# Layer 1 of a two-layer kernel: row gathers with a bound, and PSUM operands for VectorE's additions

## The chip, the cores and the metric

The kernel runs on one core of a Trainium2 chip. The metric is the time of one execution on the device in microseconds, as the median of several. The times in the profile come from one execution taken by the hardware profiler. Engine names in the profile: PE is the matrix multiplier (TensorE), PEld its loading of weights, DVE is VectorE, ACT is ScalarE, POOL is GpSimd, SP the engine that issues most DMAs; a small q (ACTq, SPq) is the queue of an engine. L853 is line 853 of the kernel.

## The reference

The input is 32 images of 128 channels and 56 x 56 pixels, all in float32. There are two layers.

Layer 0 is a depthwise 7 x 7 convolution and a layer norm over the channels, followed by a mixture of eight experts. Each of the T = 32 x 56 x 56 = 100,352 pixels is a token, and chooses its two best experts. An expert takes at most `cap = 1.25 T / 8 = 15,680` choices, in the order of the first choice's weight; what comes later is dropped and gets slot `E * cap`, which is a row of zeros:

```python
pos = take_along_axis(cumsum(oneh, axis=0) - 1, tiF[:, None], axis=1)[:, 0]
keep = pos < cap
slot = where(keep, tiF * cap + pos, E * cap)
y = einsum('ecf,efd->ecd', gelu(einsum('ecd,edf->ecf', eb, W1) + b1), W2) + b2
yf = concatenate([y.reshape(E * cap, C), zeros((1, C))], axis=0)
contrib = yf[slot] * gate[:, None]      # two rows of yf for each token
x = input + x_skip + layer_scale * (contrib summed over the two choices)
```

Layer 1 takes this x. It makes `feat`, a dilated 3 x 3 convolution down to 64 channels with batch norm and gelu, and its two-dimensional Fourier transform F2. One half of the output's channels is the absolute value of the inverse transform of an attention over the channels, the other that of the inverse transform of F2 times a sigmoid gate. Both are added to x:

```python
out_f = abs(ifft2(einsum('bhde,bhen->bhdn', attn, F2)))
gate = abs(ifft2(sigmoid(...) * F2))
return concatenate([out_f, gate], axis=1) + x
```

## The kernel before

There are three stages, one after the other. The first makes the convolution of layer 0, the norm and the choice of experts, and writes the normed tokens to `xf` in DRAM. The second lists the tokens of each expert, gathers them (`xg`, L674) and runs the experts; their rows, already multiplied by gate and layer scale, go to `yf` in DRAM. `yf` has NSLOT = 125,440 rows and one more, which is filled with zeros from `zrow` (L389 to L391). `slot1` and `slot2` hold for each token the row of its first and second choice, or NSLOT where the choice was dropped. The third stage is layer 1, and the change lies there.

The third stage works on pairs of images, sixteen of them. The image pair is laid out as two padded tiles `xps[0]`, `xps[1]` of 128 channels, and `feat` holds both images' 64 channels in 128 partitions. Two generators are woven together. `front` makes the x of the next pair and its `feat`; `back` does the Fourier part of the present pair. The main loop runs a step of `front` whenever `back` has done its share of matmul columns (`goal`). The order of instructions on each engine is fixed when the kernel is built; it follows this weaving roughly, not line by line.

`front` goes over seven row blocks of a pair (r counts them over all pairs, 112 in all). For each block there are four things:

- `gather(r)` loads seven times 128 tokens of `xf` as `xs` (L848), and for each of the two choices seven gathers of 128 rows from `yf` into a tile `y` (L853). A gather is an indirect DMA that GpSimd issues; its row numbers are one column of `slot1` or `slot2`. The `y` tiles come from a pool of four, so two blocks are in flight.
- `total(r)` adds the two `y` tiles to `xs` on VectorE (L867), which frees them.
- `place(r)` transposes `xs` on TensorE into PSUM (`pxs`, L875) and adds it into `xps` on VectorE (L880).
- `taps` does the 3 x 3 convolution as matmuls (`pf`, L898), with gelu on ScalarE into `feat` (L906).

`feed(rb)` in `front` calls `place(r)`, `total(r + 1)` and `gather(r + 3)` in that order.

`back` has four transforms, each of which transposes (`pt`, L934), copies to SBUF on VectorE (`mid`, L936), multiplies (`pm`, L942) and copies out, mostly on ScalarE (L945, L1020). Between the second and the third stand the attention weights (`gb`, `at_`, `attn`) and seven calls of `attend(g)`: two matmuls `pre` and `pim` (L1032, L1033), a square of each on ScalarE into `sr` and `si` (L1036, L1037), and the addition of both on VectorE into `feat` (L1038). There too lie the gate (`gt`, L1088) and the sums and differences X, Y and Q (L1057 to L1061, L1091 to L1097). Beside the third transform, `attended(g)` takes the root of `feat` on ScalarE for each image into `oa` (L1046), adds x on VectorE (L1049) and stores. After the fourth transform, `absolute` takes the absolute value of each image's half of `pm` on ScalarE into `ob` (L1122), adds x on VectorE (L1126) and stores.

[...] Here `bank(...)` hands out five of them in turn for `pt`, `pm`, `pre`, `pim`, `pxs` and the like; a bank is free again when its last reader is done.

Of the kernel before, what the change touches and what calls it, by code (L numbers as in the profile page):

```python
# [29 lines left out]
F32 = mybir.dt.float32  # L30
I32 = mybir.dt.int32
AF = mybir.ActivationFunctionType
ALU = mybir.AluOpType
# [4 lines left out]
C = 128  # L38
H = W = 56
RP = 59  # L40
XL = 62 * RP + 6
NQ = H * RP
INT0 = 3 * RP + 3
# [3 lines left out]
DD = 64  # L47
# [3 lines left out]
NB = H // P8  # L51
# [8 lines left out]
def interior(ap, h0, nh):  # L60

    at = INT0 + h0 * RP
    return ap[:, at : at + nh * RP].rearrange("p (h w) -> p h w", w=RP)[:, :, 0:W]
# [8 lines left out]
def conv_seq_kernel(ctx: ExitStack, tc: tile.TileContext, t: dict, out: bass.AP, dbg: dict):  # L72
    nc = tc.nc
# [4 lines left out]
    NSLOT = E * cap  # L78
# [5 lines left out]
    dram = ctx.enter_context(tc.tile_pool(name="dram", bufs=1, space=DRAM))  # L84
# [3 lines left out]
    def bank(name):  # L88
        return psum.tile([128, 512], F32, tag="bank", name=name)
# [10 lines left out]
    nc.vector.memset(eps6, 1.0e-6)  # L100

    xf = dram.tile([J * 128, PITCH], F32, name="xf")
    yf = dram.tile([NSLOT + 1, C], F32, name="yf")
    xfv = xf.rearrange("(j p) c -> p j c", p=128)


# [7 lines left out]
    with tc.tile_pool(name="a1", bufs=1) as a1, tc.tile_pool(name="a2", bufs=2) as a2, tc.tile_pool(  # L114
        name="a3", bufs=3
# [214 lines left out]
        for g in range(HI // 2):  # L330
            y = a2.tile([128, TG, C], F32, name="y")
# [31 lines left out]
    with tc.tile_pool(name="b1", bufs=1) as b1, tc.tile_pool(name="b2", bufs=2) as b2, tc.tile_pool(  # L363
        name="c1", bufs=1
# [21 lines left out]
            )  # L386
            nc.vector.tensor_tensor(out=b2v[:, e], in0=b2v[:, e], in1=lsB, op=ALU.mult)

        zrow = c1.tile([1, C], F32, name="zrow")  # L389
        nc.vector.memset(zrow, 0.0)  # L390
        nc.sync.dma_start(out=yf[NSLOT : NSLOT + 1, :], in_=zrow)  # L391

        blocks = b1.tile([128, U, NC], F32, name="blocks")
        for u in range(U):
            nc.vector.tensor_scalar(
                out=blocks[:, u, :], in0=iota[:, :NC], scalar1=float(-u), scalar2=None, op0=ALU.add
# [4 lines left out]
            out=token, in0=iota, scalar1=-128.0, scalar2=128.0, op0=ALU.add, op1=ALU.mult  # L401
# [397 lines left out]
    d2 = ctx.enter_context(tc.tile_pool(name="d2", bufs=2))  # L799
# [42 lines left out]
    rows = {}  # L842

    def gather(r):
        if r >= NRB:
            return
        xs = d3.tile([128, NB, C], F32, name="xs")
        nc.sync.dma_start(out=xs, in_=xfv[:, r * NB : (r + 1) * NB, :C])  # L848
        ys = []
        for s in (slot1, slot2):  # L850
            y = d4.tile([128, NB, C], F32, name="y")
            for m in range(NB):
                nc.gpsimd.indirect_dma_start(  # L853
                    out=y[:, m, :],
                    out_offset=None,
                    in_=yf,
                    in_offset=bass.IndirectOffsetOnAxis(ap=s[:, r * NB + m : r * NB + m + 1], axis=0),
                )
            ys.append(y)
        rows[r] = xs, ys  # L860

    def total(r):
        if r >= NRB:
            return
        xs, ys = rows[r]
        for y in ys:
            nc.vector.tensor_tensor(out=xs, in0=xs, in1=y, op=ALU.add)  # L867

    def place(r, xps):
        xs, rb = rows.pop(r)[0], r % NB  # L870
        for m0 in range(0, NB, 4):
            nm = min(4, NB - m0)
            pt = bank("pxs")
            for m in range(nm):
                nc.tensor.transpose(pt[:, m * 128 : (m + 1) * 128], xs[:, m0 + m, :], ident)  # L875
            pv = pt[:, : nm * 128].rearrange("p (m i r s) -> p i r m s", m=nm, i=2, r=P8)
            for i in range(2):
                px = interior(xps[i], rb * P8, P8)[:, :, m0 * P8 : (m0 + nm) * P8]
                px = px.rearrange("p r (m s) -> p r m s", m=nm)
                nc.vector.tensor_tensor(out=px, in0=px, in1=pv[:, i], op=ALU.add)  # L880

    def front(pr, xps, feat):


        for i in range(2):
            nc.sync.dma_start(out=xps[i], in_=t["xp"][pr + i * HI])

        def feed(rb):
            r = pr * NB + rb
            place(r, xps)  # L890
            total(r + 1)
            gather(r + 3)

        def taps(pf, g, k0):
            for k in range(k0, k0 + 3):
                o = ((k // 3) * 3 + 8 * g) * RP + (k % 3) * 3
                for i in range(2):
                    nc.tensor.matmul(  # L898
                        pf[i * DD : (i + 1) * DD, : 8 * W],
                        lhsT=cw[:, k, :],  # L900
                        rhs=xps[i][:, o : o + 8 * RP].rearrange("p (h w) -> p h w", w=RP)[:, :, :W],
                        start=(k == 0),
                        stop=(k == 8),
                    )
            if k0 == 6:
                nc.scalar.activation(  # L906
                    feat[:, 8 * g * W : 8 * (g + 1) * W], pf[:, : 8 * W], AF.Gelu, scale=bsc, bias=bsh
                )

        feed(0)  # L910
        yield NB * 64
        for g in range(NB):
            if g + 1 < NB:
                feed(g + 1)
                yield NB * 64
            pf = psumf.tile([128, 512], F32, name="pf")
            for k0 in (0, 3, 6):
                taps(pf, g, k0)
                yield 3 * 8 * W


# [37 lines left out]
    def back(pr, xps, feat):  # L959
# [67 lines left out]
        def attend(g):  # L1027

            pre = bank("pre")
            pim = bank("pim")  # L1030
            ftf = feat[:, 8 * g * W : 8 * (g + 1) * W]
            nc.tensor.matmul(pre[:, : 8 * W], lhsT=attn, rhs=ftf, start=True, stop=True)  # L1032
            nc.tensor.matmul(pim[:, : 8 * W], lhsT=meanw, rhs=ftf, start=True, stop=True)  # L1033
            sr = d2.tile([128, 8 * W], F32, name="sr")
            si = d2.tile([128, 8 * W], F32, name="si")
            nc.scalar.activation(sr, pre[:, : 8 * W], AF.Square)  # L1036
            nc.scalar.activation(si, pim[:, : 8 * W], AF.Square)  # L1037
            nc.vector.tensor_tensor(out=ftf, in0=sr, in1=si, op=ALU.add)  # L1038
            return 2 * 8 * W

        def attended(g):

            for i in range(2):
                oa = ring.tile([128, 8 * W], F32, name="oa", tag="o")
                ov = oa[:DD].rearrange("p (h w) -> p h w", w=W)
                nc.scalar.activation(  # L1046
                    oa[:DD], feat[i * DD : (i + 1) * DD, 8 * g * W : 8 * (g + 1) * W], AF.Sqrt
                )
                nc.vector.tensor_tensor(out=ov, in0=ov, in1=interior(xps[i], 8 * g, 8)[:DD], op=ALU.add)  # L1049
                nc.sync.dma_start(out=out[pr + i * HI, :DD, 8 * g : 8 * g + 8, :], in_=ov)  # L1050


# [51 lines left out]
        for i, w in enumerate(  # L1104
            transform(
                lambda k: Q[:, 2 * k : 2 * k + 2, :].rearrange("p a l -> p (a l)"), KF, 4 * KF, ih,
                lambda k, n: T4[:, 2 * k * H : 2 * (k + n) * H], act,
            )
        ):
            if i % 2 and i // 2 < NB:  # L1110
                attended(i // 2)
            yield w
# [3 lines left out]

        def absolute(at, pm):
            j0, nj = at
            for i in range(2):
                ob = ring.tile([128, 8 * W], F32, name="ob", tag="o")  # L1120
                ov = ob[DD:].rearrange("p (b j w) -> p b j w", b=2, w=W)
                nc.scalar.activation(  # L1122
                    ov, pm[i * DD : (i + 1) * DD].rearrange("p (j b w) -> p b j w", b=2, w=W), AF.Abs
                )
                px = xps[i][DD:, INT0 : INT0 + H * RP].rearrange("p (b j w) -> p b j w", b=2, w=RP)
                nc.vector.tensor_tensor(out=ov, in0=ov, in1=px[:, :, j0 : j0 + nj, :W], op=ALU.add)  # L1126
                po = out[pr + i * HI, DD:].rearrange("c (b j) w -> c b j w", b=2)
                nc.sync.dma_start(out=po[:, :, j0 : j0 + nj, :], in_=ov)

        yield from transform(  # L1130
            lambda j: T4[:, bass.DynSlice(j, 4 * KF, step=NT)], NT, 4 * KF, iw,
            lambda j, n: (j, n), absolute,
        )

# [6 lines left out]
    for r in range(3):  # L1141
        gather(r)
# [9 lines left out]
    for w in front(0, *this):  # L1152
        pass
    for pr in range(NI // 2):
        then, steps = None, iter(())
        if pr + 1 < NI // 2:
            then = pair()
            steps = front(pr + 1, *then)
        made = fed = 0
        for w in back(pr, *this):  # L1160
            made += max(w, 0)
            goal = max(0, made - LEAD) * FRONT // (MAIN - LEAD)
            if w < 0:
                goal = max(goal, fed - w * 3 * 8 * W)
            while fed < goal:
                f = next(steps, None)
                if f is None:
                    break
                fed += f
        for w in steps:  # L1170
            pass
        this = then
# [137 lines left out]
```

## Time and profile before

| | before |
|---|---|
| median of 3 runs | 5500.93 us (5497.88 to 5509.63) |
| span of the profiled execution | 5513.8 us |
| stage 3, from the first gather of `y` to the end | 3250.2 to 5513.8 us |
| gathers of `y` (L853) | 1568, mean 1045 ns, busy 1638.6 us |
| additions `xs<-xs,y` (L867) | 224, mean 1091 ns |
| `oa<-oa,xp` (L1049) and `ob<-ob,xp` (L1126) | 224 each, mean 612 and 627 ns |
| `feat<-sr,si` (L1038) | 112, mean 619 ns |
| roots (L1046) and absolute values (L1122) | 224 each, mean 576 and 538 ns |
| loads of ScalarE's table at L1046 in stage 3 | 79, 1283 ns each |

A line of the costliest groups reads: line, engine, operation, what is written from what, how often; then busy time and the mean of one; then the idle time of that engine just before these instructions, and what ended most of it. "issue" means that the engine waited for nothing that the profile shows. In the timeline, a line has the start in us, the length in us, the instruction, and in brackets the idle time before it. A line of the windows has, for each engine, busy time and number of instructions in that stretch, then the granted TensorE clock, the share of the DMA engines that is busy, and GB/s.

### The profile page before, as it was taken

What the parts mean: (1) busy time and instruction counts of PE and PEld (TensorE: products, weight loads), DVE (VectorE), ACT (ScalarE), POOL (GpSimd) and SP (SyncE); (2) the same over time, 40 slices, a digit from 0 to 9 for tenths busy, and PEclk for the clock granted to TensorE, in tenths of its full rate; (3) what the DMA queues carried; (4) which work ended last, traced back from release to release, by engine and by line L of the source; (5) the groups of instructions that cost most, each with busy time, mean ns of one, the idle gap of its engine ahead of it and who ended that gap; (6) DMA issues with size and microseconds to landing.
All of it is one profiled execution on the core that took longest, in us unless ns stands there. A gap on an engine that the chain in (4) does not pass through costs nothing.

```text
span 5513.8 us, 85629 instructions
## 1 busy us (share of the span) xinstructions
PE 4653.0 (84%) x32850; PEld 3226.8 (59%) x32850; DVE 3073.9 (56%) x6927; ACT 2097.5 (38%) x3595; POOL 2613.8 (47%) x2564
## 2 busy tenths in 40 slices
PE   6777675189988989899999965899999999899898
PEld 6666554166666667667776743555555555555556
DVE  4767776746565656454453322555555555555556
ACT  2544556023322323233333310444444444444445
POOL 0000000053535343445454447777777777777770
PEclk9888887589999999999999987999999999999999
DMA  9999995222222222222222243444444444444441
GB/s 258 247 242 244 241 233 132 50 66 60 69 54 66 57 62 61 63 66 71 69 70 73 73 120 74 118 126 127 123 123 124 125 123 123 125 128 125 123 121 42
DMA packets 616217, 634.09 MB, mean 115 GB/s; under 512 B 166145, under 2 KB 540546, under 8 KB 611714
## 3 DMA queue, kind: packets, MB, share of 16 engines
q1 hardware_dynamic: 332418, 395.64, 25.6%
q0 software_dynamic: 81664, 175.18, 14.8%
q10 hardware_dynamic: 201728, 57.81, 5.4%
q8 instruction: 260, 4.26, 0.3%
q14 instruction: 147, 1.20, 0.1%
HBM read 454.98 MB, written 173.41 MB: 114 GB/s over the span
## 4 chain that ended last, share of the span: by engine, by line
POOL 28%; PE 25%; issue 19%; DVE 7%; DMA 6%; ACT 2%; ACTq 0%; POOLq 0%; DVEq 0%; SPq 0%
POOL y L853 17%; POOL xg L674 10%; PE py L718 6%; PE ph L708 5%; PE pf L898 4%; PE pm L942 4%; DMA xg<-xf,ids 3%; DMA y<-yf,slot 2%; PE pt L934 2%; PE pg L966 1%; ACT y L181 1%; PE psa L136 1%; PE pxt L680 1%; DVE junk L419 1%; DVE y L187 1%
## 5 line engine op out<-in xcount | busy, mean ns | idle before, releaser
L853 POOL DMA_INDIRECT y<-yf,slot x1568 | 1638.6, 1045 | 527.7 <-issue 501.0
L674 POOL DMA_INDIRECT xg<-xf,ids x984 | 963.8, 979 | 1338.4 <-PE pxt L680 490.0
L711 ACT ACTIVATE hT<-ph,b1t 128x512 f32<-128x512 f32 (+1 forms) x992 | 676.1, 682 | 1428.8 <-PE ph L708 1402.6
L718 PEld LDWEIGHTS py<-W,hT 128*128 128x128 f32 x7872 | 950.8, 195 | 224.7 <-issue 155.1
L718 PE MATMUL py<-W,hT 128*128 128x128 f32 x7872 | 998.2, 281 | 75.4 <-DVE yo L731 69.8
L708 PE MATMUL ph<-xT,W 128*128 128x512 f32 (+1 forms) x1984 | 903.9, 595 | 0.2 <-DVE xT L694 0.2
L898 PE MATMUL pf<-xp,cw 128*64 128x448 f32 x4032 | 885.9, 566 | 0.9 <-DVE xp L880 0.8
L867 DVE TENSOR_TENSOR xs<-xs,y 128x896 f32<-128x896 f32 x224 | 244.4, 1091 | 644.7 <-DMA y<-yf,slot 591.9
L898 PEld LDWEIGHTS pf<-xp,cw 128*64 128x64 f32 x4032 | 289.0, 141 | 465.9 <-issue 439.7
L708 PEld LDWEIGHTS ph<-xT,W 128*128 128x128 f32 x1984 | 359.9, 193 | 336.4 <-issue 329.7
L136 PE MATMUL psa<-xt,wt 112*64 112x98 f32 x8192 | 413.1, 262 | 83.2 <-DMA wt<-in_wt_dram 74.9
L685 DVE SCALAR_TENSOR_TENSOR gat<-xg 128x4 f32<-128x4 f32 (+2 forms) x256 | 42.1, 164 | 785.0 <-DMA xg<-xf,ids 782.4
L136 PEld LDWEIGHTS psa<-xt,wt 112*64 112x64 f32 x8192 | 389.4, 146 | 121.4 <-issue 67.0
L936 DVE COPY mid<-pt 112x512 f32<-112x512 f32 (+3 forms) x480 | 305.3, 660 | 229.7 <-PE pt L934 229.0
L290 POOL MEMSET meta<- 128x1568 f32 x8 | 11.2, 1404 | 887.1 <-DMA xf<-meta 451.5
L181 ACT ACTIVATE y<-y,nb,sd 128x128 f32<-128x128 f32 x784 | 307.9, 482 | 119.1 <-issue 70.2
L945 ACT COPY T<-pm 128x464 f32<-128x464 f32 (+2 forms) x240 | 124.7, 520 | 404.7 <-PE pm L942 404.7
L144 DVE TENSOR_TENSOR y<-psa,dwbB 128x392 f32<-128x392 f32 x256 | 142.7, 563 | 232.8 <-PE psa L136 232.7
L731 DVE TENSOR_TENSOR yo<-py,b2t 128x512 f32<-128x512 f32 (+2 forms) x256 | 169.8, 666 | 112.1 <-PE py L718 111.3
L198 PE MATMUL pyt<-ident,y 128*128 128x128 f32 x784 | 137.8, 347 | 92.0 <-DVE nb L174 57.9
L680 PE MATMUL pxt<-ident,xg 128*128 128x128 f32 (+1 forms) x984 | 195.2, 280 | 11.0 <-DMA xg<-xf,ids 10.8
L1033 PE MATMUL pim<-feat,meanw 128*128 128x448 f32 x224 | 126.4, 651 | 92.2 <-ACT gt L1088 92.2
(376 smaller groups left out, 6185.1 us busy)
## 6 DMA issues: line engine op xcount, KB each, us to landing
xt<-in_x_dram SPq DMA_DIRECT2D x128, 784.0 KB
yf<-yo SPq DMA_DIRECT2D x240, 256.0 KB
xp<-in_xp_dram SPq DMA_DIRECT2D x32, 1832.0 KB
wt<-in_wt_dram SPq DMA_DIRECT2D x128, 448.0 KB
xs<-xf SPq DMA_DIRECT2D x112, 448.0 KB
xf<-y ACTq DMA_DIRECT2D x48, 1024.0 KB
y<-yf,slot POOLq DMA_INDIRECT x1568
out_dram<-oa SPq DMA_DIRECT2D x224, 112.0 KB
```

The source lines that it names most:

```text
L136: nc.tensor.matmul(ps[h * 64 : (h + 1) * 64, c * TG : (c + 1) * TG], lhsT=wt[:, c4 + c, b, :], rhs=xv[:, c4 + c, h, :, b * NB : b * NB + N ...
L181: nc.scalar.activation(yi, yi, AF.Identity, scale=sd[:, i : i + 1], bias=nb[:, i : i + 1])
L674: nc.gpsimd.indirect_dma_start(out=xg[:n, q, :], out_offset=None, in_=xf, in_offset=bass.IndirectOffsetOnAxis(ap=ids[:n, c0 + q : c0 + q + ...
L680: nc.tensor.transpose(pt[:, q * 128 : q * 128 + n], xg[:n, q, :C], ident[:n, :n])
L708: nc.tensor.matmul(ph[:, :ns], lhsT=W1[:, e, f * C : (f + 1) * C], rhs=xT[:, :ns], start=True, stop=True)
L711: nc.scalar.activation(hT[:, f, :ns], ph[:, :ns], AF.Gelu, bias=b1t[:, e, f : f + 1])
L718: nc.tensor.matmul(py[:n, q * C : (q + 1) * C], lhsT=hT[:, f, q * 128 : q * 128 + n], rhs=W2[:, e, f, :], start=(f == 0), stop=(f == FF // ...
L853: nc.gpsimd.indirect_dma_start(out=y[:, m, :], out_offset=None, in_=yf, in_offset=bass.IndirectOffsetOnAxis(ap=s[:, r * NB + m : r * NB + ...
L867: nc.vector.tensor_tensor(out=xs, in0=xs, in1=y, op=ALU.add)
L898: nc.tensor.matmul(pf[i * DD : (i + 1) * DD, : 8 * W], lhsT=cw[:, k, :], rhs=xps[i][:, o : o + 8 * RP].rearrange("p (h w) -> p h w", w=RP) ...
L936: dve(mid[:m, :ni, :].rearrange("p i c -> p (i c)"), pt[:m, : ni * 128])
L942: nc.tensor.matmul(pm[:, i * M : (i + 1) * M], lhsT=mid[:m, i, :], rhs=by, start=True, stop=True)
```

## The change

It has two parts, and one move.

The gathers get a bound: a row number above NSLOT - 1 is skipped instead of read, so a dropped choice moves nothing. What it leaves in `y` must then be zero, so ScalarE clears each `y` tile before its gathers. The row of zeros in `yf` and its writing go. The purpose is to spare the reads of dropped choices.

The squares of `pim`, the roots and the absolute values are written to PSUM rather than to SBUF: `pim` and `pm` in place, the roots into a bank of their own, `root`. VectorE's additions then read one operand from PSUM and one from SBUF. [...] a root or an absolute value is taken once over 128 partitions for both images, where it was taken twice over 64.

The move: `gather` is no longer called in `feed` but later, behind the first three taps of a row block, for the same block r + 3.

```diff
-    yf = dram.tile([NSLOT + 1, C], F32, name="yf")
+    yf = dram.tile([NSLOT, C], F32, name="yf")
...
-        zrow = c1.tile([1, C], F32, name="zrow")
-        nc.vector.memset(zrow, 0.0)
-        nc.sync.dma_start(out=yf[NSLOT : NSLOT + 1, :], in_=zrow)
...
             y = d4.tile([128, NB, C], F32, name="y")
+            nc.scalar.memzero(y)
             for m in range(NB):
                 nc.gpsimd.indirect_dma_start(
                     out=y[:, m, :],
                     out_offset=None,
                     in_=yf,
                     in_offset=bass.IndirectOffsetOnAxis(ap=s[:, r * NB + m : r * NB + m + 1], axis=0),
+                    bounds_check=NSLOT - 1,
+                    oob_is_err=False,
                 )
...
             total(r + 1)
-            gather(r + 3)
...
         feed(0)
         yield NB * 64
+        gather(pr * NB + 3)
...
                 taps(pf, g, k0)
+                if k0 == 0 and g + 1 < NB:
+                    gather(pr * NB + g + 4)
                 yield 3 * 8 * W
...
-            si = d2.tile([128, 8 * W], F32, name="si")
             nc.scalar.activation(sr, pre[:, : 8 * W], AF.Square)
-            nc.scalar.activation(si, pim[:, : 8 * W], AF.Square)
-            nc.vector.tensor_tensor(out=ftf, in0=sr, in1=si, op=ALU.add)
+            nc.scalar.activation(pim[:, : 8 * W], pim[:, : 8 * W], AF.Square)
+            nc.vector.tensor_tensor(out=ftf, in0=sr, in1=pim[:, : 8 * W], op=ALU.add)
...
+            root = bank("root")
+            nc.scalar.activation(root[:, : 8 * W], feat[:, 8 * g * W : 8 * (g + 1) * W], AF.Sqrt)
             for i in range(2):
                 oa = ring.tile([128, 8 * W], F32, name="oa", tag="o")
                 ov = oa[:DD].rearrange("p (h w) -> p h w", w=W)
-                nc.scalar.activation(
-                    oa[:DD], feat[i * DD : (i + 1) * DD, 8 * g * W : 8 * (g + 1) * W], AF.Sqrt
-                )
-                nc.vector.tensor_tensor(out=ov, in0=ov, in1=interior(xps[i], 8 * g, 8)[:DD], op=ALU.add)
+                rv = root[i * DD : (i + 1) * DD, : 8 * W].rearrange("p (h w) -> p h w", w=W)
+                nc.vector.tensor_tensor(out=ov, in0=rv, in1=interior(xps[i], 8 * g, 8)[:DD], op=ALU.add)
...
+            nc.scalar.activation(pm, pm, AF.Abs)
             for i in range(2):
                 ob = ring.tile([128, 8 * W], F32, name="ob", tag="o")
                 ov = ob[DD:].rearrange("p (b j w) -> p b j w", b=2, w=W)
-                nc.scalar.activation(
-                    ov, pm[i * DD : (i + 1) * DD].rearrange("p (j b w) -> p b j w", b=2, w=W), AF.Abs
-                )
...
-                nc.vector.tensor_tensor(out=ov, in0=ov, in1=px[:, :, j0 : j0 + nj, :W], op=ALU.add)
+                nc.vector.tensor_tensor(
+                    out=ov,
+                    in0=pm[i * DD : (i + 1) * DD].rearrange("p (j b w) -> p b j w", b=2, w=W),
+                    in1=px[:, :, j0 : j0 + nj, :W],
+                    op=ALU.add,
+                )
```

More of the change, by code (lines that the diff above doesn't have):

```diff
@@ L1121, in absolute @@
                 ov = ob[DD:].rearrange("p (b j w) -> p b j w", b=2, w=W)
-                nc.scalar.activation(
-                    ov, pm[i * DD : (i + 1) * DD].rearrange("p (j b w) -> p b j w", b=2, w=W), AF.Abs
-                )
-                px = xps[i][DD:, INT0 : INT0 + H * RP].rearrange("p (b j w) -> p b j w", b=2, w=RP)
-                nc.vector.tensor_tensor(out=ov, in0=ov, in1=px[:, :, j0 : j0 + nj, :W], op=ALU.add)
+                px = xps[i][DD:, INT0 : INT0 + H * RP].rearrange("p (b j w) -> p b j w", b=2, w=RP)
+                nc.vector.tensor_tensor(
[3 more added lines that the diff above has]
+                    op=ALU.add,
+                )
                 po = out[pr + i * HI, DD:].rearrange("c (b j) w -> c b j w", b=2)
```

## Prediction

> **What bounds the kernel now.** I read the page first (engines, slices, costliest groups), then the chain of waits in the stage that the change touches, then a table of that stage in windows, and last the timeline of single instructions.
>
> ```profile
> PE 4653.0 (84%) x32850; PEld 3226.8 (59%) x32850; DVE 3073.9 (56%) x6927; ACT 2097.5 (38%) x3595; POOL 2613.8 (47%) x2564
> ...
> L853 POOL DMA_INDIRECT y<-yf,slot x1568 | 1638.6, 1045 | 527.7 <-issue 501.0
> ```
>
> The whole-span shares point at TensorE. They mix three stages, though: only the third one, from 3250 us on, is changed, and there the second line matters: 1568 gathers of 1045 ns, with an idle time ahead of them that waits for nothing ("issue").
>
> ```profile
> core 0: us, PE busy (x) PEld busy (x) DVE busy (x) ACT busy (x) POOL busy (x), PEclk, DMA share, GB/s
> 3250.00:3500.00 250.00, 141.71 (x691) 78.29 (x692) 63.61 (x110) 34.94 (x53) 190.85 (x194) 0.75 0.38 93
> 4436.00:4569.00 133.00, 121.83 (x745) 73.82 (x745) 75.58 (x133) 59.56 (x93) 103.14 (x99) 0.96 0.50 126
> 4569.00:4703.00 134.00, 122.80 (x745) 74.13 (x745) 75.50 (x133) 59.52 (x93) 104.14 (x99) 0.95 0.50 125
> 5370.00:5514.00 144.00, 122.95 (x798) 87.43 (x798) 88.22 (x156) 78.14 (x129) 0.00 (x0) 0.91 0.18 41
> ```
>
> In the windows, one pair of images takes 133.4 us, fourteen times running. A pair has 98 gathers. From 3500 to 5367 us they start 1359.4 ns apart on average: 98 x 1.3594 = 133.2 us, which is the period itself. The gap ahead of each is 0.30 us and never shorter, so GpSimd has no slack at all. TensorE is next: 122 of 133.4 us, and its idle 10 us are mostly two waits per pair that go back to gathers (about 6 us until ScalarE's `gt` at L1088, held by `xs` adds on VectorE that wait for gathers; 3 us ahead of `pre`). VectorE waits 411.6 us in the fourteen pairs for gathers to land. Only the 147 us after the last gather are free of it.
>
> What sets the length of a gather? The timeline:
>
> ```profile
> 4575.72 0.59 DVE L1092 TENSOR_TENSOR Y<-Y,gt 128x421 f32<-128x421 f32 x1
> ...
> 4577.24 1.03 DVE L1094 TENSOR_TENSOR Q<-X 128x841 f32<-128x841 f32 x1
> ...
> 4577.43 1.65 POOL L853 DMA_INDIRECT y<-yf,slot  x1 [0.30 <-issue]
> ...
> 4585.58 3.38 DVE L1049 TENSOR_TENSOR oa<-oa,xp 64x448 f32<-64x448 f32 x6
> ...
> 4587.85 1.33 POOL L853 DMA_INDIRECT y<-yf,slot  x1 [0.30 <-issue]
> ...
> 4592.99 1.88 DVE L936 COPY mid<-pt 116x512 f32<-116x512 f32 x3
> ...
> 4594.20 0.94 POOL L853 DMA_INDIRECT y<-yf,slot  x1 [0.30 <-issue]
> ```
>
> The gather beside `Q<-X` (two inputs, both in SBUF) takes 1.65 us, the one beside `oa<-oa,xp` (again two in SBUF) 1.33, the one beside a copy out of PSUM 0.94. I counted this over the fourteen pairs, 1374 gathers: the 723 that overlap no VectorE instruction with two SBUF inputs take 943 ns each, with 0.3 us over that in all; the 651 that do carry the whole excess, 152 us. Shared out by overlap, it is 54.0 us to `xs<-xs,y` (L867), 25.7 to `oa<-oa,xp` (L1049), 17.4 to `ob<-ob,xp` (L1126), 14.2 to `feat<-sr,si` (L1038), and 40 to the X, Y and Q operations.
>
> [...] adds start some 2 us after the last gather of their tile has ended. So fewer bytes alone do not shorten these 943 ns. [...]
>
> **The change part by part.**
>
> *Operands in PSUM.* `feat<-sr,pim`, `oa<-root,xp` and `ob<-pm,xp` each read one input from PSUM instead of two from SBUF. Their 35 instructions a pair no longer lengthen gathers: 25.7 + 17.4 + 14.2 = 57.3 us over fourteen pairs, 4.1 a pair. VectorE's own time stays (0.61 to 0.63 us an add here; copies out of PSUM take 0.69 for 512 columns). The `xs` adds and the X, Y, Q operations stay, and so do their 94 us.
>
> *ScalarE.* Seven roots over 128 partitions replace fourteen over 64 (0.576 us each: -4.0 us a pair), seven absolute values replace fourteen (0.538: -3.8). The built order of instructions shows 131 table loads instead of 225, six fewer a pair: -7.5. Added: 14 clears of 128x896. ScalarE's copies take 0.25 us for 112 columns and 0.53 for 448, so 0.83 ns a column and about 0.90 us a clear: +12.6. Sum -2.7 on 59.5 us of 133: ScalarE is hidden before and after.
>
> *The wait that the clears add.* A gather now waits for a clear, and the clear stands in ScalarE's queue behind `xs` adds. Behind it in that queue are the copies `Q`, the squares and `gt`, for which TensorE waits. In before, a `y` buffer comes free 5.5 us or more (median 24) ahead of the first gather that reuses it, so about 0.9 us of clearing plus its place in the queue fits. The tightest place is the fourth row block of a pair: there the built order sets four clears between the four `Q` copies. The buffer is free 6.3 us ahead; the clear ends about 1.4 us after, and the last `Q` copy is delayed by about 2 us. Both hide as long as the gathers bound the pair. Moving `gather` behind the first taps only changes the order in which things are queued.
>
> *PSUM banks held longer.* `pm` is held by one activation and two adds (about 1.8 us) instead of two activations (1.1), and `root` takes a sixth user of five banks. A step of the transforms takes two banks, so TensorE runs about two steps ahead, some 3 us; it may lose a few us a pair, inside the 6 to 9 us that it gains when gathers come earlier.
>
> *The skip.* Choices: 2 x 100,352 tokens = 200,704; slots 8 x 15,680 = 125,440; so at least 37.5% of the rows, 48 of 128 in a gather, are skipped (from the shapes). Before, they all read the zero row. Their bytes weigh nothing, DMA is at half share. What counts is GpSimd's time per gather, and no gather of before has a bound. Low end: a skipped row costs as little as an absent one. The eight gathers of 64 rows in the second stage take 903 to 906 ns against 943 for 128: 40 ns for 64 rows, so 30 ns saved. [...] I take zero, a compare that eats what the skipped rows save.
>
> Each ns counts 1568 times, 1.57 us. Sum: 5500.9 - 57.3 + 0 = 5443.6. The pair goes to 129.2 us and is still GpSimd's: 98 x (1.013 + 0.305).
>
> **The rivals.**
>
> *Skipped rows shorten the gather by 30 ns.* Another 1568 x 0.030 = 47 us: 5397. The pair would be 126.3 us, just above what TensorE needs (133.4 less 10 idle, about 124), so little more can come. For it: rows cost something in the 64-row gathers. Against: little[...].
>
> *The bound costs 80 ns a gather.* +125 us: 5569, slower. [...]
>
> *The new waits take the gain.* Clears in ScalarE's queue or banks held longer stop TensorE, or gathers start late by about 4 us a pair: 5500, no change. For it: four clears between the `Q` copies. Against: ScalarE is 45% busy and the slack is 20 us in most places.
>
> **How the numbers follow.** 0.42 for the forecast, 0.25 for the shorter gather, 0.24 for the dearer one, 0.09 for the new waits. Predicted 5444. The range runs from 5385 (shorter gathers and a few us in the last 147) to 5575 (80 ns more)[...]. Faster: 0.42 + 0.25 + a third of the last = 0.70. Within 0.2%: 0.05. Slower: 0.25.
>
> **What would show it.** The mean of a gather: 1010 ns as forecast, 980 in the first rival, 1090 in the second. Its shortest: 943 if the test is free. The timeline beside `oa` and `ob`: 0.94 us gathers. The pair's window: 129 us with the 0.30 us gap before each gather. A gap that grows with ScalarE as its releaser would show the new waits, TensorE idle on ScalarE or VectorE the held banks. Wrong at the root would be gathers that stay long beside PSUM adds, or a length that has nothing to do with VectorE.

## The result, and the profile after

The changed kernel takes 5541.87 us (median of four executions, 5534.33 to 5551.94) where the kernel before takes 5499.68 on the same chip: a ratio of 1.0074, 95% interval 1.0054 to 1.0095. It is slower by about 42 us. The profiled executions are 28 us apart (5541.7 and 5513.8), because the one of before, an execution of 5515.6 us, was slower than any of its timed runs; traces are compared with those 28 us.

From the page of the changed kernel: the engines, the queue that carries the gathers, and the groups of the gather and of the clear (busy us, mean ns | idle us ahead and what ended most of it).

```profile
PE 4690.9 (85%) x32850; PEld 3232.8 (58%) x32850; DVE 3098.7 (56%) x6926; ACT 2040.4 (37%) x3501; POOL 2648.5 (48%) x2564
...
q0 software_dynamic: 81664, 136.94, 9.6%
...
L852 POOL DMA_INDIRECT y<-yf,slot x1568 | 1673.5, 1067 | 527.0 <-issue 469.0
...
L850 ACT ACTIVATE y<-y 128x896 uint32<-128x896 uint32 x224 | 212.3, 949 | 644.7 <-DVE xs L868 620.5
```

The skip does what it is for. The queue of the gathers moves 136.94 MB instead of 175.18; 38.24 MB at 512 bytes a row are 74.7 thousand rows not read, some 37% of them. And yet a gather has become longer on average, 1067 ns instead of 1045. The idle time ahead of the gathers is what it was (527.0 and 527.7 us): nothing new is waited for. The waits of GpSimd in the last stage say so directly (us in total, times, longest us):

```profile
POOL y L852 <- issue: 419.3, 1376, 0.3
POOL y L852 <- DMA y<-yf,slot: 46.6, 153, 0.3
POOL y L852 <- ACT y L850: 5.3, 17, 0.4
```

Only 5.3 us are put down to the clears, in waits hardly longer than the gap of 0.3 us that stands ahead of every gather anyway. So the time is in the gathers themselves. All instructions of that line, shortest, median and longest in ns:

```profile
L852 POOLq MOVE  x1568: 29/29/35, 3193.5 to 5388.0; - x196
L852 POOL DMA_INDIRECT y<-yf,slot x1568: 992/997/2499, 3246.6 to 5396.6; - x196
```

Before, the same line read:

```profile
L853 POOL DMA_INDIRECT y<-yf,slot x1568: 938/944/2397, 3250.2 to 5366.3; - x196
```

The shortest has moved up by 54 ns, the median by 53. The MOVE of 29 ns is new; every run with a bound has it and none without. It lies in the gap, which stays 0.30 us. A pair in the windows, columns as in the prediction:

```profile
core 0: us, PE busy (x) PEld busy (x) DVE busy (x) ACT busy (x) POOL busy (x), PEclk, DMA share, GB/s
4436.00:4569.00 133.00, 123.38 (x737) 73.56 (x733) 77.17 (x133) 55.03 (x86) 103.65 (x97) 0.96 0.37 107
4569.00:4703.00 134.00, 123.01 (x746) 73.43 (x745) 77.27 (x133) 55.59 (x88) 104.08 (x98) 0.97 0.36 107
```

Gathers now start 1378.3 ns apart over the fourteen pairs, 98 x 1.3783 = 135.1 us a pair instead of 133.2. ScalarE has 4 us less a pair, and the DMA share has gone from 0.50 to 0.37, and neither shortens the pair: GpSimd is still what it waits for.

From the timeline, the PSUM edit at work (L1040) and what it left (L868):

```profile
4440.47 0.62 DVE L1040 TENSOR_TENSOR feat<-sr,pim 128x448 f32<-128x448 f32 x1 [1.97 <-ACT pim L1039]
4440.57 1.00 POOL L852 DMA_INDIRECT y<-yf,slot  x1 [0.30 <-issue]
...
4470.43 1.09 DVE L868 TENSOR_TENSOR xs<-xs,y 128x896 f32<-128x896 f32 x1 [2.29 <-DMA xs<-xf]
4470.63 1.76 POOL L852 DMA_INDIRECT y<-yf,slot  x1 [0.30 <-issue]
...
4609.93 0.99 POOL L852 DMA_INDIRECT y<-yf,slot  x1 [0.31 <-DMA y<-yf,slot]
4610.01 1.09 DVE L868 TENSOR_TENSOR xs<-xs,y 128x896 f32<-128x896 f32 x1 [4.09 <-DMA y<-yf,slot]
```

The gather at 4440.57 begins with 0.52 us of an addition still to run and takes 1.00 us, the new bare time (that of a gather which meets no addition with two SBUF inputs). Over the fourteen pairs 144 gathers begin well inside an addition with a PSUM operand (0.05 us or more into it, at least 0.15 us left) and meet none with two SBUF inputs; they take 997 ns on average and 1013 at most. In before the 142 that began so inside `oa`, `ob` or `feat` took 1257 on average. The additions themselves take what they took: `oa` 617 ns and `ob` 622 on average (224 of each), against 612 and 627 with both inputs in SBUF; for one image of each pair the operand in PSUM lies in other partitions than the output (0 to 63 and 64 to 127). The gather beside `xs` at 4470.63 takes 1.76 us. The `xs` addition at 4610.01, on the other hand, cost nothing: the gather that had begun at 4609.93 took 0.99.

Over the fourteen pairs the excess above the bare time fell from 152 us to 106. A lengthened gather ends a fixed time after the end of an addition with two SBUF inputs (the last section has the figures), so its excess can be put down to that one addition. Counted like this:

| us of excess in fourteen pairs | `oa`, `ob`, `feat` | `xs` | X, Y, Q |
|---|---|---|---|
| before | 45.9 | 65.9 | 39.7 |
| changed | 0 | 72.5 | 33.6 |

Against the 46 us that the excess fell stand 53 ns on 1374 gathers, 73 us. For all 1568 gathers the sum of durations went from 1638.6 to 1673.5 us, +34.9, and the time from the first gather's start to the last one's from 2116.0 to 2150.0, +34.0. The stretch after the last gather lost 2.5 us and the stages ahead of the first 3.6; that makes the 28.

### The profile page after: what moved, and what is told of

Its sections match the earlier page's. It is cut to its first block, busy times and chain, and to the rows that moved or that the text cites. A ratio compares the mean times of both kernels' runs of the same rounds, so it can differ in the third digit from the quotient of the medians.

```text
span 5541.7 us, 87589 instructions
## 1 busy us (share of the span) xinstructions
PE 4690.9 (85%) x32850; PEld 3232.8 (58%) x32850; DVE 3098.7 (56%) x6926; ACT 2040.4 (37%) x3501; POOL 2648.5 (48%) x2564
## 3 DMA queue, kind: packets, MB, share of 16 engines
q0 software_dynamic: 81664, 136.94, 9.6%
## 4 chain that ended last, share of the span: by engine, by line
POOL 26%; issue 25%; PE 16%; DMA 11%; DVE 5%; ACT 1%; POOLq 1%; ACTq 0%; DVEq 0%; SPq 0%
POOL y L852 16%; POOL xg L671 10%; DMA y<-yf,slot 8%; PE py L715 6%; PE ph L705 5%; DMA xg<-xf,ids 3%; PE pf L898 1%; PE pm L945 1%; ACT y L181 1%; PE pxt L677 1%; DVE junk L416 1%; PE pt L937 0%; POOLq L852 0%; DVE y L187 0%; PE pyt L198 0%
## 5 line engine op out<-in xcount | busy, mean ns | idle before, releaser
L852 POOL DMA_INDIRECT y<-yf,slot x1568 | 1673.5, 1067 | 527.0 <-issue 469.0
L898 PE MATMUL pf<-xp,cw 128*64 128x448 f32 x4032 | 909.6, 566 | 0.5 <-DVE xp L881 0.5
L868 DVE TENSOR_TENSOR xs<-xs,y 128x896 f32<-128x896 f32 x224 | 245.0, 1094 | 555.6 <-DMA y<-yf,slot 476.6
L850 ACT ACTIVATE y<-y 128x896 uint32<-128x896 uint32 x224 | 212.3, 949 | 644.7 <-DVE xs L868 620.5
```

Source lines behind the costliest of these rows:

```text
L850: nc.scalar.memzero(y)
L852: nc.gpsimd.indirect_dma_start(out=y[:, m, :], out_offset=None, in_=yf, in_offset=bass.IndirectOffsetOnAxis(ap=s[:, r * NB + m : r * NB + ...
L898: nc.tensor.matmul(pf[i * DD : (i + 1) * DD, : 8 * W], lhsT=cw[:, k, :], rhs=xps[i][:, o : o + 8 * RP].rearrange("p (h w) -> p h w", w=RP) ...
```

## The experiments

Theory A, after the result: the last stage lasts as long as GpSimd's gathers; the bound adds 53 ns to each whatever it skips; the PSUM edits take off what the additions held back. Rivals: the clears or the moved call cost the time, or something other than the gathers sets it.

The chips differed, and this has to be known to read the times. Where the kernel before takes about 5500 us (the chip of the result and that of i1), TensorE has 0.94 to 0.95 of its clock in the last stage. On the chips of the other runs the kernel before takes 6344 to 6425 us; in the traces of the runs there the first two stages take some 20 to 40 us more than in before's, and the last one, where none of its matmuls is left out, 31 to 42% longer, at 0.80 to 0.85 of the clock. The changed kernel itself, with all its matmuls, was not run on such a chip. There the durations of single gathers can be read, but the whole times follow something else. The e runs shared one chip, the f runs another, the h runs a third, the n runs a fourth; i1 and i2 had one each. Ratios are to the kernel before on the same chip.

| run | us, median | ratio, 95% interval | gather, median ns | mean ns |
|---|---|---|---|---|
| e1 | 6420.07 | 1.0120 (1.0088 to 1.0152) | 945 | 1006 |
| e2 | 6256.7 | 0.9859 (0.9823 to 0.9894) | 997 | 1083 |
| e3 | 6321.69 | 0.9967 (0.9950 to 0.9984) | 997 | 1062 |
| e4 | 6398.8 | 1.0073 (1.0048 to 1.0099) | 997 | 1062 |
| f1 | 6454.75 | 1.0056 (1.0037 to 1.0076) | 945 | 1003 |
| f2 | 6290.87 | 0.9798 (0.9767 to 0.9828) | 997 | 1092 |
| f3 | 6418.46 | 1.0011 (0.9994 to 1.0028) | 997 | 1059 |
| f4 | 6489.83 | 1.0114 (1.0087 to 1.0142) | 945 | 1003 |
| i1 | 5486.65 | 0.9949 (0.9932 to 0.9965) | 947 | 1024 |
| i2 | 6416.44 | 0.9995 (0.9978 to 1.0012) | 997 | 1052 |

**e1, e2: half of the change each.** e1 is the changed kernel without the skip:

```
-            nc.scalar.memzero(y)
...
-                    bounds_check=NSLOT - 1,
-                    oob_is_err=False,
```

with the zero row put back. e2 is the changed kernel with the old squares, roots and absolute values. Both keep the gather call at its new place.

> The changed kernel without bound and clears: dropped choices read the zero row again; PSUM operands and the moved gather call stay. Theory A (the bound costs about 53 ns in every gather, the PSUM operands save what VectorE's two-SBUF additions held up): shortest gathers back at 943 ns, mean about 1010 ns, 5440 to 5460 us, 40 to 60 below the kernel before. Theory B (banks held longer and the moved call cost, the bound is harmless): gathers as after at about 1.07 us in step, or TensorE idle on banks, 5530 us or more.

> The kernel before with bound, clears and the moved gather call, but the squares, roots and absolute values in SBUF as before. Theory A: shortest gather 996 ns, the contention of before on top, mean about 1105 ns, pair about 138 us, 5575 to 5590 us. Theory B (the PSUM part is what costs): 5500 us or less, gathers below 1054 ns.

**e3, e4: parts of the skip.** e3 keeps the zero row and sets the bound where no row exceeds it, so that nothing is skipped; e4 takes only the clears out, and rows that are skipped then keep old data.

```
# e3
-                    bounds_check=NSLOT - 1,
+                    bounds_check=NSLOT,
# e4
-            nc.scalar.memzero(y)
```

> The changed kernel with a bound of NSLOT and the zero row kept, so that every row passes the bound and none is skipped; clears stay. Theory A1 (the test of the bound is what costs): shortest gather 990 to 1030 ns, the higher end if a skipped row saves time, 5540 to 5590 us. Theory A2 (a skipped row is what costs): shortest gather 943 ns, 5440 to 5470 us.

> The changed kernel without the clears of y on ScalarE, so rows of dropped choices keep what an earlier gather left there. Theory A: ScalarE was hidden, gathers stay at 996 ns and up, 5535 to 5545 us. Theory C (the clears in ScalarE's queue hold TensorE or the gathers up): 5500 us or less.

The gather line of e1 and that of e3:

```profile
L854 POOL DMA_INDIRECT y<-yf,slot x1568: 938/945/2149, 3284.2 to 6246.8; - x196
```

```profile
L855 POOLq MOVE  x1568: 29/29/35, 3228.7 to 6152.9; - x196
L855 POOL DMA_INDIRECT y<-yf,slot x1568: 991/997/2418, 3281.8 to 6162.0; - x196
```

Without the bound 938 and 945 ns, with it 991 and 997, and e3 skips no row at all. So some 53 ns are the price of having a bound. Rows that are skipped, on balance, neither save nor cost anything that shows: e3, which fetches all, and the changed kernel and e4, which skip 37%, have one duration, 997 ns in the median. That the cost is in the instruction is shown; what it is worth in the whole is not, since these whole times go against theory A (e2, with the longest gathers, is the fastest of the four, and e3 is faster than e1 though its gathers are longer). What happens there is seen in e1. Its windows from 4300 to 4347 us, and two lines of ScalarE's timeline there:

```profile
core 0: us, PE busy (x) PEld busy (x) DVE busy (x) ACT busy (x) POOL busy (x), PEclk, DMA share, GB/s
4300.00:4319.00 19.00, 17.93 (x113) 11.02 (x112) 8.08 (x16) 6.88 (x11) 14.74 (x15) 1.00 0.23 48
4319.00:4331.00 12.00, 7.44 (x15) 1.83 (x14) 1.71 (x3) 0.00 (x0) 9.33 (x9) 0.72 0.34 87
4331.00:4347.00 16.00, 0.00 (x0) 0.00 (x0) 0.00 (x0) 0.00 (x0) 10.37 (x11) 0.60 0.23 49
```

```profile
4315.05 0.55 ACT L1023 COPY Q<-pm 128x464 f32<-128x464 f32 x1 [3.63 <-remote]
4347.34 0.55 ACT L1023 COPY Q<-pm 128x464 f32<-128x464 f32 x1 [31.74 <-remote]
```

For 16 us TensorE, VectorE and ScalarE start nothing. ScalarE waits 31.74 us for the semaphore of a matmul that the records put at 4315 us; it arrives 0.02 us ahead of the copy. GpSimd goes on by itself for eleven gathers and then waits for VectorE: 930 us over the run, where all its waits beyond the gap, after the first gather, come to 0.8 us in before. Stretches of more than 4 us in which none of the three runs an instruction add up from 3260 us on to 397 us in e1, 198 in e2, 311 in e3 and 363 in e4, and to 22 and 17 in the traces of before and of the changed kernel. The clock in the records is either 1.0 or 0.5; in the traces of before and of the changed kernel it stays at one of them for multiples of 3.41 us. In the windows above it falls with TensorE's work, from 1.00 where TensorE is busy 17.93 of 19 us to 0.72 at 7.44 of 12 and 0.60 at none; and in the last stage of n1 to n4 below, where TensorE has no work at all, it is 0.50 (3400 to 5300 us). The low clock may thus come from the standing still and need not be its cause; which of the two brings on the other was not shown. Why these chips stand still is open, and so is why e2 gains there and e1 loses.

**f1 to f3: the same again on another chip.** The same edits as e1, e2 and e3. The text for f1 says that the call is at its old place; as in e1 it is at the new one.

> The same kernel as e1_psum_only: the kernel before with the PSUM edits alone (no bound, no clears, the gather call at its old place), for a chip that grants TensorE about 0.94 of its clock in the last stage instead of the 0.82 of the first call. Theory A (the last stage lasts as long as GpSimd needs for its 1568 gathers): gathers keep their 943 ns, those beside the root and absolute-value additions lose their excess of 57 us, the xs additions give back some ten of it: 45 to 55 us less, ratio 0.990 to 0.992. Theory B (the rate of the last stage is set by TensorE and what waits for it, and PSUM operands lengthen VectorE's and ScalarE's part of that): no gain or a loss of up to 1 per cent, as in the first call. If the chip again grants about 0.82, both expect 1.01 as before and the run tells nothing of A.

> The same kernel as e2_skip_only: the kernel before with the skip alone (bound, clears and the moved gather call, no PSUM edits). A: 53 ns on each of 1568 gathers is 83 us, the VectorE operations keep their excess of about 150 us: 70 to 95 us more than before, ratio 1.013 to 1.017. B: the 38 MB not moved count, and the gathers are hidden: same or faster, as in the first call (0.986).

> The same kernel as e3_bound_none_skipped: the changed kernel with the bound set so high that no row is skipped, the zero row kept and fetched, the clears kept. A: what a gather costs is the test, not the rows: 996 ns a gather again and the time of the changed kernel, ratio 1.006 to 1.009. B: the rows that are now moved (38 MB) cost time: 1.015 or more.

On that chip the engines stood still too: from 3260 to 6200 us TensorE is busy 2063 of 2940 us in f1, where it is 1846 of 2100 in before (3260 to 5360). The runs repeat what e1 to e3 showed, the gathers' 945 and 997 ns included, and their times go against A as there: the skip alone is 2% faster than the kernel before, the PSUM edits alone 0.6% slower.

**f4: `xs` additions in halves.**

```
-            nc.vector.tensor_tensor(out=xs, in0=xs, in1=y, op=ALU.add)
+            for a, b in ((0, 4), (4, NB)):
+                nc.vector.tensor_tensor(out=xs[:, a:b, :], in0=xs[:, a:b, :], in1=y[:, a:b, :], op=ALU.add)
```

> f1_psum_only with each of the 224 xs additions of 128x896 cut in two (128x512 and 128x384). In the traces a gather is only lengthened by a two-SBUF addition that runs when the gather begins, and by exactly what is left of that addition less 0.127 us. A: with the phases of the kernel before, halves leave 39 of the 66 us that the xs additions cost: 20 to 30 us less than f1, ratio about 0.986. Rival: the second half gets in before the waiting gather, and nothing is saved: the time of f1.

f4 took 35 us more than f1, where A expected 20 to 30 less. The excess that `xs` causes fell only from 61 us in f1 to 53 (1414 gathers from 3500 us on, counted by the addition whose end the gather follows), the other additions caused 12 us more, and the gathers' sum stayed (1572.0 and 1573.3 us). So the rival is right about the gathers: nothing is saved. Of the gathers that began 0.07 to 0.3 us into a half, nearly all waited for that half alone (0.30 to 0.50 us longer). Of those that began about 0.35 us into it, some waited 0.20 us for this half, some 0.68 for the next one too, and some 1.75 for all four that stood in line. So the text above, by which only an addition that runs as the gather begins counts, is too narrow: some gathers ended only behind the second half, or behind all four, and cutting an addition up doesn't shorten them for certain. The whole time belongs to a chip that stands still.

**h1 to h4: fewer matmuls.** Three of nine taps, in the kernels before, changed, e1 and e2:

```
-            for k in range(k0, k0 + 3):
+            for k in range(k0, k0 + 1):
...
-                        stop=(k == 8),
+                        stop=(k == 6),
```

> The kernel before with three of the nine convolution taps of the last stage left (k = 0, 3, 6; the other six, 2688 of the 4032 pf matmuls, are left out, so its result is another), so that TensorE, which the two chips used so far held back to 0.80 to 0.85 of its clock in that stage, is far from being the bound. Theory A (GpSimd's gathers set the time of the last stage): the period of a pair is 98 gathers of about 1.36 us as on the first chip, 133 us, and the whole about 5480 us whatever clock is granted. Theory B (TensorE and its consumers set it): well below 130 us a pair.

> The changed kernel with the same six taps left out. A: 30 to 45 us more than h1_lite_before, as on the first chip (42 us). B: at most the same as h1.

> f1_psum_only (the PSUM edits alone) with the same six taps left out. A: 40 to 57 us less than h1_lite_before. B: the same as h1, or 1 per cent more as the kernels with all taps had it.

> f2_skip_only (bound, clears and moved call alone) with the same six taps left out. A: 83 us more than h1_lite_before, 70 to 95. B: the same as h1 or up to 2 per cent less, as the kernels with all taps had it.

h1 took 6152.92 us, h2 6170.07, h3 6110.98, h4 6108.34. Theory A fails on this chip: h1's gathers are spread over 2750 us, 172 a pair; h2 is 17 us above h1 where A had 30 to 45; and h4, which should have been the slowest, is the fastest. h3's 42 us less fall into A's span, but with the gathers not the bound this proves nothing. The stretches in which nothing runs on the three engines add up to 550 us in h1, more than in any e run, so fewer matmuls do not cure them.

**n1 to n4: no TensorE in the last stage.** Banks are filled once with zeros, every matmul and transpose of the stage is dropped; the kernels are before, changed, e1 and e3.

```
+    class no:
+        matmul = transpose = staticmethod(lambda *a, **k: None)
...
+    banks = [psum.tile([128, 512], F32, name=f"fix{k}") for k in range(5)]
...
+    def bank(name):
+        turn_[0] += 1
+        return banks[turn_[0] % 5]
...
-                nc.tensor.transpose(pt[:, m * 128 : (m + 1) * 128], xs[:, m0 + m, :], ident)
+                no.transpose(pt[:, m * 128 : (m + 1) * 128], xs[:, m0 + m, :], ident)
```

> The kernel before with every TensorE instruction of the last stage left out (the PSUM banks are filled once with zeros and read and written by VectorE and ScalarE as before; the result is another), since on three chips TensorE stands still for up to 30 us at a time in that stage and hides what the gathers do. Theory A: with no TensorE left, the last stage lasts as long as its 1568 gathers, whatever the chip: about 1.25 us each without contention and 1.30 to 1.38 with it, 2040 to 2160 us from the first gather to the last. Theory B (not the gathers set the time but VectorE, ScalarE or the transfers): well under 2000 us, with GpSimd waiting.

> The changed kernel with every TensorE instruction of the last stage left out. A: each gather 53 ns longer (83 us), less what the additions with a PSUM operand no longer hold back (40 to 60 us): 20 to 45 us more than n1_still_before. B: the same as n1, or less by what the bytes not moved are worth.

> f1_psum_only (the PSUM edits and the new place of the gather call; no bound, no clears) without the TensorE instructions of the last stage. A: 30 to 60 us less than n1_still_before, and 83 us less than n2_still_after. B: the same as both.

> f3_bound_none (the changed kernel, bound so high that no row is skipped) without the TensorE instructions of the last stage. A: the time of n2_still_after within 10 us, since the test costs what it costs and the rows' 38 MB are hidden. B: more than n2 by the time of those rows.

| run | us, median | sum of the gathers | GpSimd's waits beyond the gap, after the first gather | first to last gather |
|---|---|---|---|---|
| n1 (before) | 5597.52 | 1629.1 | 127.8 | 2233.9 |
| n2 (changed) | 5627.83 | 1655.8 | 124.6 | 2257.7 |
| n3 (e1) | 5604.31 | 1599.5 | 164.0 | 2240.8 |
| n4 (e3) | 5630.29 | 1658.7 | 126.0 | 2261.9 |

Without TensorE's work in the last stage the kernel before falls from 6409.74 us to 5597.52 on this chip. But n1's 2233.9 us from the first gather to the last lie outside A's 2040 to 2160: GpSimd waits. n2 is 30 us slower than n1, inside A's span. n4 equals n2 within 2.5 us: 38 MB more, the same time. n3 misses: it should have won 30 us over n1, and lost 7. Its gathers are indeed 29.6 us shorter, but GpSimd waits 36.2 us more. A pair takes 140 to 142 us (median) in n1, n2 and n3, 9 to 11 more than its gathers and their gaps need, so GpSimd waits in all of them, in n3 mostly at the same two gathers of each pair. Where a stage has such waits, a shorter gather may only make a longer wait, as in n3. So these kernels don't measure what the PSUM edits are worth, and n2's 30 us agree with A without proving it.

**i1: the PSUM edits alone, the call at its old place.** e1, and

```
             total(r + 1)
+            gather(r + 3)
...
-        gather(pr * NB + 3)
...
-                if k0 == 0 and g + 1 < NB:
-                    gather(pr * NB + g + 4)
```

> The kernel before with the PSUM edits alone and the gather call at its old place in the feed (e1, f1, h3 and n3 had it at its new place, other than the text for f1 says). On a chip that does not hold TensorE still in the last stage (granted clock there about 0.94), theory A: 40 to 57 us less than before, ratio 0.990 to 0.993, gathers of 943 ns without contention. On a chip that does (0.80 to 0.85), if the new place of the call cost what e1 and f1 lost there (0.6 and 1.2 per cent), the ratio is 1.000 or less; if the PSUM edits did, 1.006 to 1.012 again.

This chip is like that of the result (5516.67 us for the kernel before), and i1 is faster than both kernels: 0.9949, 30 us less than before. The page's group and the gather line:

```profile
L854 POOL DMA_INDIRECT y<-yf,slot x1568 | 1605.9, 1024 | 528.7 <-issue 498.4
```

```profile
L854 POOL DMA_INDIRECT y<-yf,slot x1568: 942/947/2398, 3252.5 to 5336.8; - x196
```

The sum of the gathers is 32.7 us below before's 1638.6, and first to last start takes 2084.3 us, 31.7 less. Gather time and whole time move together, one for one, on a chip of this kind. The expected 40 to 57 us were 30: the additions that now read PSUM had caused 46 us and not 57, and `xs` and X, Y, Q cost 10 more than in before (73.6 and 42.0); the bare gather, 946 ns for 943, takes another 4. That the move of the call costs nothing isn't shown; it wasn't run alone.

**i2: the bound alone, on top of i1.**

```
+                    bounds_check=NSLOT,
+                    oob_is_err=False,
```

> i1 with nothing but the bound added to its 1568 gathers, set so high that no row is skipped (zero row kept, no clears, the call at its old place). Theory A: 996 ns for a gather without contention instead of 943, 83 us more for the sum of the gathers, less what longer gathers meet of fewer additions; on a chip that grants TensorE about 0.94 in the last stage the ratio to before is then 1.005 to 1.010, against 0.995 for i1. Rival (the time of the changed kernel comes from the clears or the new place of the call): 0.995 again. On a chip that holds TensorE still in the last stage the whole says nothing, and only the duration of a gather and the stage's mean count.

```profile
L854 POOL DMA_INDIRECT y<-yf,slot x1568: 991/997/2113, 3276.2 to 6246.3; - x196
```

Two arguments, nothing skipped, no clears, the old place: 997 ns. The chip was of the other kind (6424.8 us for before), so its whole time doesn't say more. The whole price of the bound rests on i1 and the changed kernel instead: 0.9949 and 1.0074 of before, 0.0125 apart or 69 us, and their gathers differ by 1673.5 - 1605.9 = 67.6. Without contention a gather takes 946.0 ns in i1 and 996.4 in the changed kernel; 1568 x 50.4 ns are 79 us, less 10 by which the excess is smaller in the changed kernel (106 and 116 us in fourteen pairs): 69. The clears and the moved call, which the two kernels also differ by, leave nothing to explain, to within the some 15 us that the two intervals allow.

## Why the prediction was wrong

The step that failed is the term of the skip, "I take zero, a compare that eats what the skipped rows save", the + 0 in the sum. It measured +53 ns a gather, +83 us. The number lies between what was taken, zero, and the +80 of the dearer bound, and the direction was lost there: the PSUM edits' 46 us bear a bound of up to 29 ns and no more. The argument for zero set a cost of the test against a saving by the skipped rows. There is no such saving on balance: e3 skips none and has the 997 ns of the changed kernel. What is left is the price of the bound, and it is the same when nothing is skipped: 53 ns, or 0.4 ns for each of 128 rows. The +80 was my assumption, worked out from no trace; it was the nearer guess, for a reason that no run here shows.

A second term was mis-sized, "-57.3". The mechanism was right: gathers inside the three kinds of additions now take the bare 997 ns, in i1 946. But the prediction shared a gather's excess over all the additions that it overlapped, where one addition causes it. By cause the three kinds had 45.9 us and `xs` 65.9 (shared out: 57.3 and 54.0). (Of the 651 gathers counted there beside additions with two SBUF inputs, 14 lie only beside `gb<-pg,ident`, which reads PSUM; they have no excess.) The rest was not fixed either: `xs` rose by 6.6 us and X, Y, Q fell by 6.1, which happen to cancel in the changed kernel; in i1 they rose by 7.7 and 2.3. Gathers that start at other moments meet other additions. Net -46 in the changed kernel, -33 in the gathers of i1.

What held: the last stage is GpSimd's and its gathers' durations are its time (34.9 us more gather time, 34.0 us more between first and last gather). Fewer bytes gave nothing where that was tried by itself (n4 and n2). ScalarE's edits and the clears are hidden: the clear takes 949 ns instead of the estimated 900, the pair 55 us of ScalarE instead of 59.5, and GpSimd waits 5.3 us for clears in all. The wait that was feared for TensorE, on `gt`, is 101 us over fourteen pairs, 7 a pair against about 6. The rival of new waits is out. The rival of the dearer bound named the cause and 5569 us; with 53 ns for 80 and 46 us for 57 it comes near the result: 5500 + 83 - 46 is 5537.

## What to carry to other kernels

When one instruction is repeated without a gap on the engine that bounds a stage, a new option on it is the first thing to price: multiply by the count (1.57 us for each ns here) before counting what it saves elsewhere. 38 MB not moved gave nothing where that was tried by itself (n4 and n2), and the index bound that spares them cost time. Share a delay out by what ended it, not by what ran beside it. Try the halves of a change by themselves: the PSUM operands alone beat both kernels on the chip where the gathers are the bound (0.9949 against 1.0074). But this holds for that kind of chip: on the other kind these edits, with the call moved, were slower than the kernel before (1.0120 and 1.0056) and the skip alone was faster (0.9859 and 0.9798), and no run here shows why.

## What the runs showed of the hardware

A gather that was lengthened ends a fixed time after the end of a VectorE addition with two SBUF inputs: 0.87 us in the changed kernel, 0.82 in before, whose bare gather is 53 ns shorter. Within 20 ns this holds for 215 of the 220 gathers in fourteen pairs of the changed kernel that took over 10 ns more than the bare time, and for 402 of 405 in before; the others have at most 18 ns. So the excess is what is left of that addition when the gather begins, less 0.127 us. The gather at 4470.63 shows it: the addition ends at 4471.52, 0.89 us later; 0.89 - 0.13 + 1.00 = 1.76.

Mostly the addition is already running as the gather begins (some 0.05 us or more). One that VectorE begins after standing idle, later than the gather, lengthened none, as at 4610.01: of the gathers in fourteen pairs for which the first of these additions to come began so, the 75 in the changed kernel took 1001 ns at most, the 143 in before 953. But an addition that VectorE takes up directly behind another instruction can hold a gather that began before it:

```profile
3598.14 1.88 DVE L939 COPY mid<-pt 112x512 f32<-112x512 f32 x3
...
3599.39 2.49 POOL L852 DMA_INDIRECT y<-yf,slot  x1 [0.30 <-issue]
3599.93 1.08 DVE L868 TENSOR_TENSOR xs<-xs,y 128x896 f32<-128x896 f32 x1
```

This gather began 0.54 us before the addition and waited for all of it. Such `xs` additions held 17 gathers in the changed kernel (23.9 us of its 106), eleven of them at one and the same place of the pair; 6 in before (8.3 us of its 152) and 9 in i1 (10.9 us). When a following addition gets in and when it doesn't was not worked out. What in a gather waits for these additions, no trace here shows.

A bound on an indirect gather of 128 rows cost 50 to 53 ns (944 to 947 ns without it, 997 with it, in the medians of before, e1, i1, e3, i2 and the changed kernel), whether it skips none or 37% of them; the 512 bytes of a skipped row weren't moved (136.94 MB in the queue instead of 175.18), while its count of packets stayed at 81664.
